# New planned step durations, leads and limits for the order of a graph network's last stage

## The chip, the cores and the metric

The kernel runs on one core of a Trainium2 chip. The metric is the device time of one execution in microseconds (us), taken as the median of several runs. A profile of one execution gives start and end of every instruction. PE is the matrix engine (TensorE), DVE is VectorE, ACT is ScalarE, POOL is GpSimd, SP is SyncE, which here issues most DMAs. Each engine works through its own list of instructions in order; semaphores make one engine wait for another. PSUM is the small memory that PE writes to, SBUF the large one.

## What is computed

128 graphs of 128 nodes with 128 features pass through four layers of graph networks. Each layer normalizes its input, applies a relu, attends over the graph's edges and adds the result to its input:

```
h = relu(layernorm(x));  x = x + L0(h, adj)
    y = softmax(where(adj > 0, scores(|x_i - x_j|), -9e15)) @ x
    y = leaky(batchnorm(y @ Wg.T + bg), 0.01);  out = [x, y] @ Wt.T + bt
h = relu(layernorm(x));  x = x + L1(h, adj)
    8 heads of 32:  att = softmax(where(mask, leaky(f1_i + f2_j, 0.2), -9e15))
    xc = elu(att @ h_head);  h2 = xc @ W2
    one more attention over h2;  out = elu(att2 @ h2) + h
h = relu(layernorm(x));  x = x + L2(h, adj)
    one attention on h itself;  out = elu(att @ h)
h = relu(layernorm(x));  x = x + L3(h, adj)
    typed scores src_i a[edge type] dst_j;  out = softmax(leaky(scores)) @ val @ pw.T + pb
```

## The kernel before

Earlier stages (until about 1724 us of the profile) compute the pairwise differences of layer 0, its two batch statistics and its attention, and leave in DRAM the values that the rest needs. The last stage, the function `layers_01`, is all the change is about. It is the arm for edges that are 0 or 1. It does the end of layer 0 and layers 1 to 3, for 32 groups of four graphs (`GC = 4`).

A group's work is a Python generator, `group(g)`, with helpers that it calls or forks. Every `yield` in it announces the next step: the engine, the planned duration in us, the buffers that the step takes, and those that are free after it. The code up to the next `yield` issues that step's instructions. The planner `in_order` keeps up to `Z_UNDER_WAY` such generators going, and at each turn picks the step that can begin first by the planned durations, plus a hand-over of 0.2 us between engines. A table `Z_LATER` shifts the rank of a kind of step by some us (a negative number puts it ahead). `Z_KEPT` says how many buffers of a kind have to stay free for the oldest group before a younger one may take one. What the planner picks becomes the fixed order of PE, ACT, DVE and POOL in the built program. The planned times have no other effect: on the chip each instruction starts when its engine reaches it and its semaphores are met.

The steps of one group, with the lines of the profile:

- Load: four DMAs on SP (L1808): `xg`, `yt`, `ht` with 3 buffers each, the edge mask with 10.
- Layer 0's end: ACT `yl` (L1919), DVE `leaky` (L584), PE (L1925, L1928), DVE sum `x1` (L1933).
- Three times `normal` and `transposed`: DVE statistics (L1715, L1717), ACT (L1720, L1721), POOL two tensor_tensor (L1724, L1725), PE transposes (L1732), ACT copy with relu (L1735).
- Layer 1's heads: PE (L1948), DVE splits into two bf16 parts (L1957 to L1960), ACT five times (L1969), then for each of the four graphs PE scores `z` (L1821), ACT exps (L1827, L1830), DVE maximum and masking (L1832). For each pair of graphs PE `pv` (L1843), DVE `vals` (L1846), PE 64 small matmuls into `va` and `sm` (L1861), ACT (L1872, L1873), DVE `xT` (L1875). Then the elu: ACT (L1981, L1982), DVE (L1985).
- Layer 1's second attention and layer 2's attention, both in `single_head`: ACT exps (L1750 or L1747), DVE masking (L1740), PE weighted sums `po` (L1784), DVE reciprocal `ri` and product `xh` (L1791, L1793), DVE positive part plus the residual (L1774, in `positive`), ACT `ex` (L1763), DVE the sum `xo` (L1767). `own` (L2010) and `hv` (L1905) are small or medium DVE steps ahead of them. `x1h` (L1891) is the residual of layer 1.
- Layer 3: PE (L2043, L1882, L2056), ACT (L2046, L1885, L2058), PE `sel` and `other` (L2064), DVE choice by edge (L2066), ACT exps (L2069, L2070), DVE maximum (L2072), PE `po` (L1784), DVE `ri` and `xh`, POOL the sum (L2078), and the store by SP (L2079). POOL also adds the bias to the residual (L1814).

The buffers: four PSUM tiles `ps`, two double PSUM tiles `pz`, 30 SBUF tiles `t` of 128x512, 13 `w` of 128x1024, and smaller sets.

The planner's choice, in which the change acts by the numbers alone:

```
begin = max([free_at[engine], c["ready"], *(events[e] for e in c["after"])])
...
    spare = 0 if c["age"] == oldest else kept.get(kind, 0)
...
age = c["age"] if started < len(makers) else -c["age"]
rank = begin + later.get(c["key"], 0.0), age, k
```

Of the kernel before, what the change touches and what calls it, by code (L numbers as in the profile page):

```python
# [32 lines left out]
UNDER_WAY = 6  # L33
Z_UNDER_WAY = 8
Z_T, Z_W, Z_P, Z_F, Z_O, Z_M = 30, 13, 4, 4, 6, 10
Z_KEPT = {"t": 12, "w": 4, "vals": 1, "v": 3}
C_T, C_W, C_V, C_O, C_M = 28, 11, 3, 6, 7
# [32 lines left out]
Z_LATER = {  # L70
    "2": -0.5, "3": 0.3, "4": -1.2, "6": -0.3, "7": 1.5, "8": -0.4, "11": -0.4, "13": 0.3, "16":
    0.4, "21": -1.5, "25": -6.2, "28": -6.7, "29": -5.8, "32": -4.8, "34": -1.9, "36": -0.4,
    "38": -1.1, "39": 0.6, "40": -2.6, "43": 0.4, "45": -4.1, "46": -1, "47": -6.9, "48": 0.2,
    "49": -7.5, "55": -0.6, "56": 0.5, "57": -8, "58": -0.6, "59": -8, "62": -0.1, "63": 0.4,
    "0.0": -0.6, "14.2": 0.2, "14.3": -0.2, "14.4": -1.9, "14.6": -0.1, "14.0.1": -1, "14.1.2":
    -0.3, "15.3": -0.4, "15.5": -0.4, "15.6": -0.3, "15.0.1": -7.8, "15.0.2": -0.2, "15.1.1":
    0.4, "15.1.2": -0.2, "20.0": -2.2, "37.0": -0.5, "42.0": -0.1, "50.0": 4.4, "53.0": 0.2,
    "53.1": -0.2, "54.1": 0.3,
}
# [126 lines left out]
def kernel(ctx: ExitStack, tc: tile.TileContext, x, adj, w, out):  # L206
# [1468 lines left out]
    def layers_01(first_in):  # L1675

        with tc.tile_pool(name="c_in", bufs=3) as c_in, tc.tile_pool(
# [31 lines left out]
            def normal(x, out):  # L1709

                yield DVE, 1.1, "", ""
                s6 = c_s.tile([P, GC, 6], F32, tag="s6", name="s6")
                mv = c_s.tile([P, GC, 2], F32, tag="mv", name="mv")
                for g in range(GC):
                    nc.vector.bn_stats(s6[:, g, :], x[:, g, :])  # L1715
                for g in range(GC):
                    nc.vector.bn_aggr(mv[:, g, :], s6[:, g, :])  # L1717
                yield ACT, 0.47, "", ""
                rs = tile_s("rs")
                nc.scalar.activation(rs, mv[:, :, 1], AF.Ln, bias=eps_c)  # L1720
                nc.scalar.activation(rs, rs, AF.Exp, scale=-0.5)  # L1721
                yield POOL, 2.1, "t", ""
                xn = tile_t("xn")
                nc.gpsimd.tensor_tensor(xn, x, bcast(mv[:, :, 0], 2, P), ALU.subtract)  # L1724
                nc.gpsimd.tensor_tensor(xn, xn, bcast(rs, 2, P), ALU.mult)  # L1725
                out.append(xn)

            def transposed(xn, out, frees):
                yield PE, 1.0, "ps", frees
                pt = psum("pt")  # L1730
                for g in range(GC):
                    nc.tensor.transpose(pt[:, g, :], xn[:, g, :], ident)  # L1732
                yield ACT, 0.5, "t", "ps"
                t = tile_t("hTc")
                nc.scalar.activation(t, pt, AF.Relu)  # L1735
                out.append(t)
# [5 lines left out]
            def single_head(z, own, mask, least, values, ones_at, after, out):  # L1742

                yield ACT, 1.02 if own else 0.57, "t", "ps"
                t = tile_t("p")
                if own is None:
                    nc.scalar.activation(t, z, AF.Exp, bias=shift_01, scale=1.0 - SLOPE)  # L1747
                else:
                    for g in range(GC):
                        nc.scalar.activation(  # L1750
                            t[:, g, :], z[:, g, :], AF.Exp, bias=own[:, g : g + 1], scale=1.0 - SLOPE
                        )
                yield DVE, 0.62, "", ""
                masked_larger(t.rearrange(flat), mask.rearrange(flat), least)
                yield "join",
                yield PE, 1.0, "pz", "t v"
                po = weighted(t, values, ones_at + 1)
                yield DVE, 0.86, "t", "pz"
                xh = over_sums(po, ones_at)
                yield "fork", positive(xh, after, out)  # L1760
                yield ACT, 0.53, "t", ""
                ex = tile_t("ex")
                nc.scalar.activation(ex, xh, AF.Exp)  # L1763
                yield "join",
                yield DVE, 0.62, "", "t t t"
                xo = out[0].rearrange(flat)
# [4 lines left out]
            def positive(xh, after, out):  # L1771
                yield DVE, 0.63, "t", ""
                xo = tile_t("xo")
# [38 lines left out]
            def with_bias3(x3):  # L1812
                yield POOL, 1.3, "", ""
                nc.gpsimd.tensor_tensor(x3, x3, bcast(pb_bc, 1, GC), ALU.add)  # L1814

            def head_attention(i, f1d, fl, mask, es, ps_):
                yield PE, 0.34, "pz w", ""
                z, p = psum2("z"), tile_w("p")
                for s in range(2):
# [4 lines left out]
                    )  # L1824
                yield ACT, 1.13, "", ""
                z = z.rearrange("p s (h j) -> p (s h) j", h=HH)
# [3 lines left out]
                nc.scalar.activation(z, z, AF.Exp, scale=1.0 - SLOPE)  # L1830
                yield DVE, 1.1, "", "pz"
                nc.vector.scalar_tensor_tensor(p, z, 1.0, bcast(mask[:, i, :], 1, NH), ALU.max, ALU.mult)  # L1832
                ps_[i] = p

            def two_graphs(k, f1d, fl, mask, h1T, es, xT):
# [3 lines left out]
                yield "join",  # L1839
                yield PE, 0.88, "ps vals", ""  # L1840
                pv = c_ps.tile([P, 2, NH * DH], F32, tag="ps", name="pv")
                for a in range(2):
                    nc.tensor.matmul(pv[:, a, :], h1T[:, 2 * k + a, :], w1c, start=True, stop=True)  # L1843
                yield DVE, 0.6, "", "ps"
                vals = c_v.tile([P, 2 * NH, DH], F32, tag="vals", name="vals", bufs=Z_P)
# [3 lines left out]
                )  # L1849
                yield PE, 2.05, "ps ps", "w w vals"  # L1850
                va, sm = (
                    c_ps.tile([P, 2, 2, P], F32, tag="ps", name=name) for name in ("va", "sm")
                )
                for a in range(2):
                    i = 2 * k + a
                    for s in range(2):
                        for to in (va, sm):
                            for h in range(HH):
# [9 lines left out]
                                )  # L1868
                yield ACT, 1.17, "t", "ps"
                r = tile_t("r")  # L1870
                rf = r.rearrange(flat)
                nc.scalar.activation(rf, sm.rearrange("p a s n -> p (a s n)"), AF.Ln)  # L1872
                nc.scalar.activation(rf, rf, AF.Exp, scale=-1.0)  # L1873
                yield DVE, 0.61, "", "ps t"
                nc.vector.tensor_tensor(  # L1875
# [3 lines left out]
            def type_scores(t, h3T, dstT, by_type):  # L1879
                yield PE, 0.82, "ps", ""  # L1880
                pp = psum("pp")
# [6 lines left out]
            def with_h1(xn, x1, res):  # L1888
                yield DVE, 0.89, "t", "t t"
                x1h = tile_t("x1h")  # L1890
# [5 lines left out]
            def scaled(ph2, h2):  # L1896
                yield ACT, 0.95, "", "pz"
                for i in range(GC):
# [4 lines left out]
            def relu_scaled(hv, xn):  # L1903
                yield DVE, 0.82, "", "t"
                nc.vector.scalar_tensor_tensor(  # L1905
# [3 lines left out]
            def group(g):  # L1909
# [5 lines left out]
                res = {}  # L1915
                yield ACT, 0.72, "t", ""
                xg, mask, yt, ht = loaded.pop(g)
                yl = tile_t("yl")
                nc.scalar.activation(yl, yt, AF.Identity, bias=y_bi, scale=y_sc)  # L1919
                yield DVE, 0.82, "", ""  # L1920
                leaky(nc.vector, yl.rearrange(flat), yl.rearrange(flat), 0.01)
                yield PE, 1.9, "ps", "t"
                po = psum("po0")
                for i in range(GC):
# [5 lines left out]
                    )  # L1930
                yield DVE, 0.66, "t", "ps " + in_slot
                x1 = tile_t("x1")
# [12 lines left out]
                for i in range(GC):  # L1945
                    for s in range(2):
# [4 lines left out]
                        )  # L1951
                yield DVE, 1.85, "", "ps"
                fa = c_v.tile([P, 2 * P], BF16, tag="fa", name="fa")
# [6 lines left out]
                nc.vector.scalar_tensor_tensor(f, fb, parts_m[:, 1:2], pff, ALU.mult, ALU.add)  # L1960
                yield ACT, 2.47, "f w", ""
                es = c_s.tile([P, GC, NH], F32, tag="es", name="es")
# [15 lines left out]
                yield "join",  # L1978
                yield ACT, 2.15, "w", "f t"
                u = tile_w("u")  # L1980
                nc.scalar.activation(u, xT, AF.Exp)  # L1981
                nc.scalar.activation(u, u, AF.Relu, bias=one, scale=-1.0)  # L1982
                yield DVE, 1.15, "", "w"
                uf, xf = (t.rearrange("p k n -> p (k n)") for t in (u, xT))
                nc.vector.scalar_tensor_tensor(uf, uf, -1.0, xf, ALU.mult, ALU.max)  # L1985

                yield PE, 2.1, "pz v", "w"
                h2 = tile_v("h2")
# [11 lines left out]
                yield "fork", scaled(ph2, h2)  # L2000
                yield PE, 0.95, "ps", ""
                z = psum("z2")
                for i in range(GC):
# [3 lines left out]
                    )  # L2007
                yield DVE, 0.35, "", ""
                own = tile_s("own")
# [8 lines left out]
                h2T = got.pop()  # L2018
                yield PE, 1.85, "ps", "t"
                z = psum("z3")  # L2020
                nc.tensor.matmul(z, a1bc, h2T, start=True, stop=False)
                for i in range(GC):
                    nc.tensor.matmul(
                        z[:, i, :], h2T[:, i, :], a2c.to_broadcast([P, P]), start=False, stop=i == GC - 1
                    )
                yield ACT, 0.15, "v", ""
                hv = tile_v("hv")
# [27 lines left out]
                for i in range(GC):  # L2055
                    nc.tensor.matmul(pv[:, i, :], h3T[:, i, :], vpw, start=True, stop=True)  # L2056
                yield ACT, 0.48, "", "ps"
                nc.scalar.copy(val[:, :, 0:P], pv)  # L2058
                yield "join",
                yield PE, 1.88, "ps ps", "t t"  # L2060
                sel, other = psum("sel"), psum("other")
# [8 lines left out]
                nc.scalar.activation(q, sel, AF.Exp, scale=SLOPE)  # L2070
                yield DVE, 0.76, "", "t"
                nc.vector.tensor_tensor(p, p, q, ALU.max)  # L2072
                yield PE, 1.0, "pz", "t v"
                po = weighted(p, val, P + 1)
                yield DVE, 0.86, "t", "pz"
                xh = over_sums(po, P)
                yield POOL, 1.45, "", "t t"
                nc.gpsimd.tensor_tensor(xh, xh, x3, ALU.add)  # L2078
# [510 lines left out]
```

## Time and profile before

| What | us |
|---|---|
| Median of 3 runs (2614.23 to 2618.11) | 2615.92 |
| The profiled execution's own time | 2615.94 |
| Its span, first to last instruction | 2614.1 |
| The last stage in it, from about 1724 to the last store | 890 |

Over the whole span PE is busy 93%, DVE 92%, ACT 83% and POOL 62%; in the last stage these shares differ, and only they count here. DMA is busy for 14% of the last stage. A group line of the profile names line, engine, operation, tiles and shapes, then the count, the busy time, the mean ns of one, and the idle time of the engine just before, with what ended it. DVE instructions overlap by some 80 ns in the records, so that the time from one start to the next is a little shorter than the duration that is shown.

Where a group is named by its number in the texts, its first output is computed in that order, 0 to 31. From group 8 to group 23 one group ends every 26.65 us.

### The profile page before, as it was taken

What the parts mean: (1) busy time and instruction counts of PE and PEld (TensorE: products, weight loads), DVE (VectorE), ACT (ScalarE), POOL (GpSimd) and SP (SyncE); (2) the same over time, 40 slices, a digit from 0 to 9 for tenths busy, and PEclk for the clock granted to TensorE, in tenths of its full rate; (3) what the DMA queues carried; (4) which work ended last, traced back from release to release, by engine and by line L of the source; (5) the groups of instructions that cost most, each with busy time, mean ns of one, the idle gap of its engine ahead of it and who ended that gap; (6) DMA issues with size and microseconds to landing.
All of it is one profiled execution on the core that took longest, in us unless ns stands there. A gap on an engine that the chain in (4) does not pass through costs nothing.

```text
span 2614.1 us, 51526 instructions
## 1 busy us (share of the span) xinstructions
PE 2434.2 (93%) x19584; PEld 1526.1 (58%) x19595; DVE 2410.7 (92%) x4638; ACT 2158.5 (83%) x3537; POOL 1633.1 (62%) x922
## 2 busy tenths in 40 slices
PE   7999999999999999799999999978888888898887
PEld 3443444444444443377787877756667777676766
DVE  9999999999999999698889888779899999999996
ACT  8999999999999999566666666558888888888875
POOL 8999999999999999654434444112333333333334
PEclk9999999999999999899999999989999999999999
DMA  3000000000000000232322232040011111111000
GB/s 106 25 25 25 25 25 25 25 25 25 25 25 25 25 21 9 79 100 94 98 86 85 93 97 70 15 146 10 27 48 46 48 46 48 38 56 38 14 10 27
DMA packets 135732, 122.62 MB, mean 47 GB/s; under 512 B 10865, under 2 KB 102450, under 8 KB 135474
## 3 DMA queue, kind: packets, MB, share of 16 engines
q1 hardware_dynamic: 134754, 118.89, 14.8%
q8 instruction: 158, 2.59, 0.4%
q14 instruction: 100, 0.82, 0.1%
q10 hardware_dynamic: 720, 0.33, 0.0%
HBM read 73.05 MB, written 46.14 MB: 46 GB/s over the span
## 4 chain that ended last, share of the span: by engine, by line
PE 48%; DVE 42%; ACT 5%; issue 3%; POOL 2%; DMA 0%; DVEq 0%; ACTq 0%; POOLq 0%
PE ph L789 19%; DVE d L759 9%; DVE six L801 7%; PE pl L1125 6%; DVE p L1832 5%; PE diff L1070 4%; PE ph L1083 3%; DVE s L1715 3%; DVE xh L1793 2%; PE sp L1093 2%; DVE p L1740 2%; DVE xo L1774 2%; DVE vals L1846 1%; DVE xT L1875 1%; DVE xo L1767 1%
## 5 line engine op out<-in xcount | busy, mean ns | idle before, releaser
L764 POOL TENSOR_TENSOR d<-he 128x2016 f32<-128x2016 f32 (+1 forms) x272 | 961.0, 3560 | 17.7 <-PE ph L789 15.1
L789 PE MATMUL ph<-d,w1T 128*64 128x512 f32 (+1 forms) x4096 | 912.4, 596 | 16.2 <-DVE six L801 9.8
L768 ACT ACTIVATE d<-d 128x2048 f32<-128x2048 f32 (+1 forms) x448 | 832.9, 1887 | 18.9 <-POOL d L764 17.8
L789 PEld LDWEIGHTS ph<-d,w1T 128*64 128x64 f32 x4096 | 323.2, 136 | 545.5 <-issue 471.0
L759 DVE SCALAR_TENSOR_TENSOR d<-pt,he 128x2048 f32<-128x2048 f32 x240 | 543.3, 2271 | 4.6 <-PE ph L789 4.4
L801 DVE BATCH_NORM_STATS2 six<-ph 128x6 f32<-128x512 f32 (+1 forms) x704 | 438.1, 677 | 11.7 <-PE ph L789 11.6
L1724 POOL TENSOR_TENSOR xn<-xo,mv 128x512 f32<-128x512 f32 x64 | 78.9, 1232 | 310.3 <-DVE mv L1717 243.2
L1056 POOL TENSOR_TENSOR base<-base,own_d 128x512 f32<-128x512 f32 x32 | 41.9, 1309 | 204.9 <-PE ph L1083 130.0
L795 ACT ACTIVATE ph<-ph 128x1008 f32<-128x1008 f32 x160 | 159.6, 998 | 11.1 <-PE ph L789 10.8
L1125 PE MATMUL pl<-its,it 128*128 128x128 f32 x1280 | 167.7, 279 | 0.0
L1079 ACT ACTIVATE d<-diff 128x640 f32<-128x640 f32 x128 | 90.0, 703 | 88.4 <-PE diff L1070 88.4
L1125 PEld LDWEIGHTS pl<-its,it 128*128 128x128 f32 x1280 | 152.8, 191 | 16.6 <-DVE s L1104 4.4
L1832 DVE SCALAR_TENSOR_TENSOR p<-z,mask 128x1024 f32<-128x1024 f32 x124 | 149.3, 1208 | 2.7 <-PE sm L1861 1.5
L1070 PE MATMUL diff<-inc,h 128*128 128x320 bf16 x768 | 128.4, 303 | 9.7 <-POOL h L1017 5.2
L1115 ACT CAST it<-pi 128x640 f32<-128x640 bf16 x128 | 86.4, 691 | 61.2 <-PE pi L1112 61.2
L1861 PE MATMUL va<-p,vals 128*32 128x128 f32 x2048 | 105.7, 277 | 29.8 <-DVE vals L1846 27.3
L1830 ACT ACTIVATE z<-z 128x1024 f32<-128x1024 f32 x128 | 129.0, 1008 | 4.1
L982 DVE SCALAR_TENSOR_TENSOR inc<-in_row,row 128x8 bf16<-128x8 f32 (+12 forms) x512 | 126.5, 315 | 0.3 <-PE in_row L973 0.2
L1725 POOL TENSOR_TENSOR xn<-xn,rs 128x512 f32<-128x512 f32 x96 | 120.0, 1250 | 8.8 <-ACT es L1827 1.0
L1724 POOL TENSOR_TENSOR xn<-x,mv 128x512 f32<-128x512 f32 x32 | 36.2, 1130 | 135.1 <-PE sm L1861 72.6
L1118 DVE TENSOR_TENSOR its<-pi,s 128x640 f32<-128x640 bf16 x128 | 101.9, 809 | 16.4 <-ACT it L1115 16.3
L2078 POOL TENSOR_TENSOR xh<-xh,xo 128x512 f32<-128x512 f32 x32 | 49.4, 1547 | 106.1 <-PE pt L1732 53.0
(326 smaller groups left out, 5234.8 us busy)
## 6 DMA issues: line engine op xcount, KB each, us to landing
ht<-h SPq DMA_DIRECT2D x64, 256.0 KB, 2.7
n<-ln_xn SPq DMA_DIRECT2D x32, 256.0 KB, 2.3
h<-he SPq DMA_DIRECT2D x32, 256.0 KB, 2.6
adj<-in_adj SPq DMA_DIRECT2D x32, 256.0 KB, 3.0
xn<-n SPq DMA_DIRECT2D x32, 256.0 KB, 2.6
xb<-in_x SPq DMA_DIRECT2D x32, 256.0 KB, 3.2
xb<-xb SPq DMA_DIRECT2D x32, 256.0 KB, 2.0
xg<-xb SPq DMA_DIRECT2D x32, 256.0 KB, 3.0
```

Of the source, the lines that this page charges most:

```text
L759: nc.vector.scalar_tensor_tensor(dv, own, 0.0, later, ALU.max, ALU.max if is_larger else ALU.subtract)
L764: nc.gpsimd.tensor_tensor(dv, later, own, ALU.subtract)
L768: nc.scalar.activation(d[:, 0 : 4 * n], d[:, 0 : 4 * n], AF.Abs, accum_out=sums[:, g, k : k + 1] if on_act else None,)
L789: nc.tensor.matmul(ph[64 * a : 64 * a + 64, t, 0:n], wt, x_, start=part == 0, stop=not is_larger or part == 3,)
L795: nc.scalar.activation(ph[:, :, 0:n], ph[:, :, 0:n], AF.Square, accum_out=squares[:, g, k : k + 1])
L801: nc.vector.bn_stats(six[g][:, 2 * by_bn.index((i, q)) + t, :], ph[:, t, 0:n])
L982: nc.vector.scalar_tensor_tensor(inc[:, :, e : e + n], in_row[:, :, 0:n], float(k + 1), row[:, :, 0:n], ALU.is_equal, ALU.subtract,)
L1070: nc.tensor.matmul(diff[:, a, 0 : SLOT_N // 2], h[:, i, :], inc[:, a * SLOT_N // 2 : (a + 1) * SLOT_N // 2], start=m == 0, stop=m == 2,)
L1125: nc.tensor.matmul(made["pl"][:, i, :], it[:, k, :], its[:, k, :], start=k == 0, stop=k == 4)
L1725: nc.gpsimd.tensor_tensor(xn, xn, bcast(rs, 2, P), ALU.mult)
L1830: nc.scalar.activation(z, z, AF.Exp, scale=1.0 - SLOPE)
L1832: nc.vector.scalar_tensor_tensor(p, z, 1.0, bcast(mask[:, i, :], 1, NH), ALU.max, ALU.mult)
```

## The change

Nothing but numbers of the planner change. No step, tile or buffer count is another.

- `Z_UNDER_WAY`: up to 11 groups at once instead of 8.
- `Z_KEPT`: the buffers held back for the oldest group: `t` 12 to 1, `w` 4 to 3, `v` 3 to 2, `vals` 1 to none, and one each of `ps`, `f` and `in`, which had none.
- `Z_LATER`: all shifts are new; their keys are places in a group's sequence of steps.
- The planned durations of most steps.

```diff
-Z_UNDER_WAY = 8
+Z_UNDER_WAY = 11
-Z_KEPT = {"t": 12, "w": 4, "vals": 1, "v": 3}
+Z_KEPT = {"ps": 1, "t": 1, "w": 3, "f": 1, "v": 2, "in": 1}
...
 Z_LATER = {
-    "2": -0.5, "3": 0.3, "4": -1.2, "6": -0.3, "7": 1.5, "8": -0.4, "11": -0.4, "13": 0.3, "16":
...
+    "1": 0.1, "4": -0.3, "6": 0.4, "7": 1.1, "8": -0.3, "9": -0.2, "11": -0.1, "13": 0.3, "16":
...
 def normal
-                yield POOL, 2.1, "t", ""
+                yield POOL, 2.35, "t", ""
 def transposed
-                yield PE, 1.0, "ps", frees
+                yield PE, 0.55, "ps", frees
 def single_head
-                yield ACT, 1.02 if own else 0.57, "t", "ps"
+                yield ACT, 1.13 if own else 0.63, "t", "ps"
-                yield DVE, 0.62, "", ""
+                yield DVE, 0.95, "", ""
-                yield DVE, 0.86, "t", "pz"
+                yield DVE, 0.8, "t", "pz"
-                yield DVE, 0.62, "", "t t t"
+                yield DVE, 0.7, "", "t t t"
 def positive
-                yield DVE, 0.63, "t", ""
+                yield DVE, 0.95, "t", ""
 def two_graphs
-                yield PE, 2.05, "ps ps", "w w vals"
+                yield PE, 1.87, "ps ps", "w w vals"
 def with_h1
-                yield DVE, 0.89, "t", "t t"
+                yield DVE, 0.62, "t", "t t"
 def relu_scaled
-                yield DVE, 0.82, "", "t"
+                yield DVE, 0.66, "", "t"
 def group
-                yield DVE, 0.82, "", ""
+                yield DVE, 0.66, "", ""
-                yield ACT, 2.15, "w", "f t"
+                yield ACT, 1.97, "w", "f t"
-                yield DVE, 0.35, "", ""
+                yield DVE, 0.2, "", ""
-                yield DVE, 0.76, "", "t"
+                yield DVE, 0.83, "", "t"
```

Some twenty more durations move by 0.01 to 0.18 us in the same way. In the old program DVE's instructions repeat themselves exactly, group after group, from group 8 to group 30. In the new one no two groups have the same surroundings; neighbouring groups often stand in pairs, with the same step of both back to back.

## The prediction

> **What bounds the kernel now.** The change touches only the last stage. I read first the busy time by stretches, cut where the picture changes: its start, its repeating middle, its end.
>
> ```profile
> 1724.00:1864.00 140.00, 114.26 (x1375) 91.87 (x1376) 120.83 (x269) 112.97 (x244) 38.39 (x33) 0.93 0.22 70
> 1864.00:2477.00 613.00, 540.88 (x6347) 432.35 (x6346) 585.67 (x1287) 513.24 (x1124) 233.04 (x207) 1.00 0.15 43
> 2477.00:2590.00 113.00, 100.20 (x1009) 77.34 (x1008) 97.83 (x221) 84.39 (x190) 48.78 (x43) 1.00 0.04 11
> 2590.00:2614.10 24.10, 13.52 (x105) 12.02 (x103) 8.58 (x16) 6.43 (x12) 6.15 (x6) 0.87 0.17 49
> ```
>
> Columns: length, then busy us of PE, weight loads, DVE, ACT, POOL; PE's granted clock; DMA. In the middle DVE is busy 585.67 of 613.00 us (95.5%), ACT 83.7%, POOL 38%. So DVE sets the pace. Its idle time by stretch is 19.2, 27.3, 15.2 and 15.5 us: 77 us, about 15 us of it hand-over gaps of under 0.25 us. I then asked what DVE's waits ended on, from 1724 us on (total us, times, longest):
>
> ```profile
> DVE ri L1791 <- PE po L1784: 20.5, 27, 1.3
> DVE sel L2066 <- PE other L2064: 11.6, 4, 8.5
> DVE x L1933 <- PE po L1928: 8.9, 7, 3.4
> ```
>
> The first is the middle's one wait, once per group; the second lies in the end, the third in the start. The timeline of DVE, and below it of POOL, over one period (start, duration):
>
> ```profile
> 2204.92 1.76 DVE L1740 SCALAR_TENSOR_TENSOR p<-p,mask 128x512 f32<-128x512 f32 x1
> 2206.61 0.68 DVE L584 SCALAR_TENSOR_TENSOR yl<-yl 128x512 f32<-128x512 f32 x1
> 2208.00 0.18 DVE L1791 RECIPROCAL ri<-po 128x4 f32<-128x4 f32 x1 [0.71 <-PE po L1784]
> ...
> 2219.87 1.52 DVE L1774 SCALAR_TENSOR_TENSOR xo<-xh,x1h 128x512 f32<-128x512 f32 x1
> ...
> 2231.59 1.76 DVE L1740 SCALAR_TENSOR_TENSOR p<-p,mask 128x512 f32<-128x512 f32 x1
> ```
> ```profile
> 2204.54 1.59 POOL L2078 TENSOR_TENSOR xh<-xh,xo 128x512 f32<-128x512 f32 x1 [3.77 <-PE pt L1732]
> ...
> 2219.48 1.37 POOL L1725 TENSOR_TENSOR xn<-xn,rs 128x512 f32<-128x512 f32 x1
> ```
>
> The period is 2231.59 - 2204.92 = 26.67 us, and 23 of them are the middle. After the masking (L1740) PE needs 1.32 us (2206.68 to 2208.00) before `ri`; one 0.68 us instruction covers it, 0.71 us stays idle. The second sight is that L1740 and L1774 take 1.76 and 1.52 us where they start while a POOL instruction runs. By groups (count | busy, mean ns | idle before):
>
> ```profile
> L1740 DVE SCALAR_TENSOR_TENSOR p<-p,mask 128x512 f32<-128x512 f32 x62 | 74.6, 1205 | 0.2 <-ACT p L1750 0.2
> L1774 DVE SCALAR_TENSOR_TENSOR xo<-xh,x1h 128x512 f32<-128x512 f32 x32 | 43.1, 1345 | 0.1
> L2072 DVE TENSOR_TENSOR p<-p,q 128x512 f32<-128x512 f32 x32 | 29.7, 929 | 2.4 <-ACT q L2070 2.4
> L1774 DVE SCALAR_TENSOR_TENSOR xo<-xh,xo 128x512 f32<-128x512 f32 x32 | 22.6, 708 | 0.1
> ```
>
> The undisturbed duration is 0.69 us. Mean less 0.69, times count: 32.1 + 21.0 + 7.6 + 0.6 us, with L1767, L1905, L584 and L1891 about 70 us in all: collisions with POOL cost as much as all DVE waits.
>
> **The change part by part.** No instruction is added, removed or resized: the same 8,800 or so stand in both programs, with 25 us of DVE time per group. Only their order on each engine changes. I laid DVE's instructions in both orders, gave each its mean start-to-start time in the profile (0.60 for a free 128x512, 1.20 for L1740, 1.14 for 128x1024, 1.06 for one normalization's statistics), and summed what stands between the two ends of each round trip through another engine.
>
> *Waits in the middle.* `ri` needs 1.32 us after the second masking. Old order: 25 of 32 groups have too little between, and the trace shows 17.7 us for it. New order: 8 groups are short, by 3.4 us together. Gain 14.3 us, taken off the path since DVE sets the end. The `ri` of the third attention (needs 1.25 after L2072): short by 1.1 us before, 6.0 after, nearly all of it in the last five groups. Scores from `leaky` to `x1` (2.96): 6.9 before, 7.7 after. The nine other round trips that are short anywhere (L1846 to L1875, L1960 to L1832, L2066 to L2072, L1717 to L1905 and to L1957, and such) together fall from 14.6 to 7.2. Sum: -14.3 + 4.9 + 0.8 - 7.4 = -16.0 us. How far such sums can be trusted: for the old order they give 36.8 us, where all DVE waits of the trace but those for L2066 come to 44. Most covers grow with eleven groups to choose from: L2010 to the first L1740 was 4.2 us in the middle and is now 3 to 46. The instructions late next are the five last groups' L2072 and `ri`.
>
> *End.* From the last statistics to `sel` takes at least 18.4 us (group 31). Between them DVE had 5.2 us of other work in the old order; the last group of the new (27) has 8.3. That would give 3.1 us, but five groups instead of four end together, and group 30 took 25.6 us in that crowd. I take 0, bounds -3 and +3.
>
> *Queues.* My sums let PE and ACT serve at once. The old order repeats itself group for group, so their queues fit once fitted; the new one never repeats. Nearest rows: ACT's five L1969 take 2.5 us in a piece, PE's 64 L1861 about 1.9. If one DVE instruction per group waits half of the old 0.71 us, 32 x 0.36 = 11 us; if none, 0. I take +4, since ACT has 16% idle in the middle.
>
> *Collisions.* Of the seven kinds that can collide, 112 instructions of 320 took over 0.85 us, costing 0.63 us each (70.8 / 112). By position in the order I get 114 for the old program, and 140 for the new (129 to 154 with POOL's starts shifted by up to 2 us). 26 more would cost 16 us. But if I sum the rest of the POOL instruction running when each one begins (1.04 us undisturbed, as L1724 at 2218.36), the old order gives 71.5 and the new 60 to 87, with mean 71. I take +2, bounds -11 and +16.
>
> The Trainium skill, "SBUF — State Buffer", section "SBUF: two separate sides", states that DVE instructions with two SBUF inputs and GpSimd ones hold the shared port as an exclusive lock for the whole instruction, the loser blocking fully. The 1.52 us of L1774 agree. The rule speaks against this change: the planner books one mean (0.95 us) for what is 0.69 or up to 1.76. By it alone, 26 new losers that each wait for a whole instruction would be +27 us, and the sum a loss of about 15.
>
> *Moved DMAs.* With 11 groups under way instead of 8, SP's loads shift. The mask has 10 buffers: in the new order at least 28 us pass from one's release to its next use, against 2.2 us to land. The others have at least 7.4 us against 3.0. POOL's queue: from statistics to L1905 takes 8.6 us; the smallest cover is 9.2. I cost these at 0; without that cover each would be a wait of its landing time, once.
>
> Sum: -16 + 0 + 4 + 2 = -10 us. The profiled execution took 2615.94 us (span 2614.1, 1.8 around it), the median of the runs is 2615.92: the same. So 2606.
>
> **The rivals.**
>
> *The wait moves (no change).* Queues take 11 and the end 3: -16 + 11 + 3 + 2 = 0, so 2616. For it: no engine's work falls, ACT is 84% busy. Against it: nearly all covers grow well beyond what a 0.7 us slip eats. This is also the case in which the plan's durations don't fit: it books 0.95 us for L1740, whose rows say 0.69 or 1.76.
>
> *Collisions decide (slower).* For it: L1767 collided 6 times of 64 in the trace, and in the new order 28 of them stand where POOL runs. With 26 more in all at a whole POOL instruction of 1.04 us, 27 us, against -16 + 4: +15, so 2631. It decides from 12 us, some 19 more at 0.63. Against it: places drawn at random would give less than the trace has, since POOL's 8 x 1.04 us fill 0.31 of a period and half an instruction is left on average: 320 x 0.31 x 0.52 = 52 us.
>
> *All of it (much faster).* Queues 0, collisions -11: 2616 - 16 - 11 = 2589.
>
> **How the numbers follow.** About 0.2%, 5 us, is what a measurement here can tell from no change. Forecast (2597 to 2611) 0.48, all of it 0.10, wait moves 0.17, collisions 0.25. Faster 0.58, same 0.17, slower 0.25. The bounds of the terms, all at their low and all at their high ends, are -16 - 3 + 0 - 11 = -30 and -16 + 3 + 11 + 16 = +14, so 2586 and 2630; they hardly come together, so 8 in 10 lie in 2589 to 2626. The forecast's own range is 2597 to 2611.
>
> **What would show it.** Right: `ri` waiting on `po` falls from 20.5 to under 9 us; DVE over 97% busy in the middle, with no period; L1740's mean near 1.1 and L1767's up from 0.76, all seven kinds together 60 to 87 us over 0.69. Wrong: DVE waits of more than 1 us on ACT's `z`, `u` or `f1d` in the middle, or an excess over 85 us. A start stretch longer than 150 us would mean that eleven groups at once jam the queues, which I costed at nothing.

## The result

The changed kernel takes 2606.31 us (median of 6 runs, 2604.11 to 2609.11) against 2614.85 us before (6 runs, 2614.11 to 2618.11). The ratio is 0.9965, 95% interval 0.9954 to 0.9975. The predicted time, 2606, is met to 0.3 us. What the trace shows behind it is not what was predicted. All waits together were forecast at -12 us (-16 + 0 + 4) and rose by 10.7; collisions were forecast at +2 us and fell by 20.2. Two terms were wrong with opposite signs and cancelled, so that the time was met this closely is luck.

The profiled execution of the changed kernel took 2609.11 us (span 2607.3), 6.8 less than the one of before. Its last stage, cut at the same times as before (length, then busy us of PE, weight loads, DVE, ACT, POOL; PE's clock; DMA):

```profile
1724.00:1864.00 140.00, 116.49 (x1549) 94.06 (x1551) 122.90 (x273) 109.87 (x235) 31.52 (x29) 0.87 0.26 80
1864.00:2477.00 613.00, 567.09 (x6408) 446.44 (x6399) 578.89 (x1290) 523.89 (x1147) 230.52 (x206) 0.99 0.13 39
2477.00:2590.00 113.00, 105.27 (x843) 82.69 (x842) 89.85 (x221) 81.41 (x182) 56.68 (x51) 1.00 0.06 17
2590.00:2607.30 17.30, 5.87 (x42) 5.10 (x40) 4.85 (x10) 3.07 (x6) 4.60 (x3) 0.69 0.19 53
```

In the middle DVE is busy for 578.89 of 613.00 us: 94.4%, where it was 95.5%, and where over 97% was forecast. So DVE waits more than before, not less. PE's granted clock in the first stretch is 0.87, where it was 0.93, but DVE's idle time there fell, from 19.2 to 17.1 us. Its waits in the last stage (total us, times, longest):

```profile
DVE ri L1791 <- PE po L1784: 18.9, 26, 1.8
DVE sel L2066 <- PE other L2064: 9.2, 9, 3.6
DVE x L1933 <- PE po L1928: 8.4, 5, 3.4
DVE hv L1905 <- ACT hv L2028: 6.8, 10, 1.3
DVE p L1832 <- ACT z L1830: 6.1, 13, 1.6
DVE vals L1846 <- PE pv L1843: 4.8, 6, 2.2
DVE xT L1875 <- ACT r L1873: 4.5, 9, 1.6
```

The first was 20.5 us and should have come under 9. `sel` fell from 11.6 and `x` from 8.9. Below them stand waits on ACT and PE that before were small (`xT` 1.9 us; `hv`, the masking L1832 on `z`, and `vals` 1.0 each). What became cheaper is DVE's own instructions. The groups that can collide with POOL (count | busy, mean ns | idle before):

```profile
L1740 DVE SCALAR_TENSOR_TENSOR p<-p,mask 128x512 f32<-128x512 f32 x62 | 47.0, 764 | 0.0
L1774 DVE SCALAR_TENSOR_TENSOR xo<-xh,x1h 128x512 f32<-128x512 f32 x32 | 24.2, 759 | 0.3
L1774 DVE SCALAR_TENSOR_TENSOR xo<-xh,xo 128x512 f32<-128x512 f32 x32 | 30.6, 963 | 0.1
L1767 DVE SCALAR_TENSOR_TENSOR xo<-ex,xo 128x512 f32<-128x512 f32 x64 | 50.6, 797 | 1.6 <-ACT ex L1763 0.5
L2072 DVE TENSOR_TENSOR p<-p,q 128x512 f32<-128x512 f32 x32 | 26.1, 816 | 2.4 <-ACT q L2070 2.3
L584 DVE SCALAR_TENSOR_TENSOR yl<-yl 128x512 f32<-128x512 f32 x31 | 28.8, 941 | 0.0
L1891 DVE SCALAR_TENSOR_TENSOR x1h<-xn,x 128x512 f32<-128x512 f32 x32 | 30.0, 939 | 0.0
...
L1985 DVE SCALAR_TENSOR_TENSOR u<-u,xT 128x1024 f32<-128x1024 f32 x32 | 43.3, 1352 | 2.6 <-ACT u L1982 2.5
...
L2010 DVE TENSOR_SCALAR own<-g 128x4 f32<-128x4 f32 x32 | 10.9, 339 | 0.0
```

The masking L1740 fell from a mean of 1205 ns to 764: 74.6 to 47.0 us, the largest single gain of the change. L1774 after `x1h` fell from 1345 to 759. Five kinds that hardly collided before do now: L584, L1891 and L1774 after `xo` (710, 708 and 708 ns before), and L1985 and L2010 (1232 and 238 before), which the prediction did not count.

Over the whole stage, from DVE's first instruction of it to its last:

| us | before | changed | difference |
|---|---|---|---|
| length | 881.6 | 875.9 | -5.7 |
| DVE busy | 813.0 | 797.2 | -15.8 |
| DVE idle | 68.6 | 78.7 | +10.2 |
| waits of over 0.25 us, with 2.85 just ahead of the first instruction | 55.8 | 66.5 | +10.7 |
| collisions: time over 0.69 us of the seven kinds | 70.8 | 50.6 | -20.2 |
| of 320 instructions, those over 0.85 us | 112 | 75 | -37 |

The collisions can be read instruction by instruction. DVE's timeline of the changed kernel, and below it POOL's (start, duration):

```profile
2096.76 0.68 DVE L1774 SCALAR_TENSOR_TENSOR xo<-xh,x1h 128x512 f32<-128x512 f32 x1
2097.96 1.15 DVE L1905 SCALAR_TENSOR_TENSOR hv<-xn,hv 128x512 f32<-128x512 f32 x1 [0.52 <-ACT hv L2028]
2099.03 1.53 DVE L1767 SCALAR_TENSOR_TENSOR xo<-ex,xo 128x512 f32<-128x512 f32 x1
2100.48 0.68 DVE L584 SCALAR_TENSOR_TENSOR yl<-yl 128x512 f32<-128x512 f32 x1
```
```profile
2096.92 1.64 POOL L2078 TENSOR_TENSOR xh<-xh,xo 128x512 f32<-128x512 f32 x1 [1.47 <-DVE xh L1793]
2098.53 1.49 POOL L1724 TENSOR_TENSOR xn<-x,mv 128x512 f32<-128x512 f32 x1
```

L1774 comes first and takes its free 0.68 us, although POOL's L2078 begins inside it. L2078 pays: it ends at 2098.56, which is the end of L1774 (2097.44) plus its own undisturbed 1.04 us and a little. L1905 begins inside L2078 and ends 0.55 us after it. L1724 begins inside L1905 and ends 0.91 us after it, and L1767 ends 0.54 us after L1724 (2100.02). So whoever comes second waits until the other's instruction has ended, and shows this time as busy. Of all 112 slow instructions before and all 75 after, POOL's was the first. In 60 overlaps before and 44 after DVE's was the first, and it lost nothing.

### The profile page after: what moved, and what is told of

It is laid out like the page before. It is cut to its first block, busy times and chain, and to the rows that moved or that the text cites. A ratio compares the mean times of both kernels' runs of the same rounds, so it can differ in the third digit from the quotient of the medians.

```text
span 2607.3 us, 51594 instructions
## 1 busy us (share of the span) xinstructions
PE 2460.5 (94%) x19595; PEld 1540.8 (59%) x19595; DVE 2394.9 (92%) x4638; ACT 2160.4 (83%) x3537; POOL 1630.7 (63%) x922
## 5 line engine op out<-in xcount | busy, mean ns | idle before, releaser
L789 PE MATMUL ph<-d,w1T 128*64 128x512 f32 (+1 forms) x4096 | 911.1, 595 | 16.6 <-DVE six L801 9.8
L1725 POOL TENSOR_TENSOR xn<-xn,rs 128x512 f32<-128x512 f32 x96 | 113.6, 1183 | 185.3 <-ACT rs L1721 173.3
L1724 POOL TENSOR_TENSOR xn<-xo,mv 128x512 f32<-128x512 f32 x64 | 77.4, 1209 | 159.9 <-DVE mv L1717 106.8
L795 ACT ACTIVATE ph<-ph 128x1008 f32<-128x1008 f32 x160 | 159.7, 998 | 11.0 <-PE ph L789 10.8
L1125 PEld LDWEIGHTS pl<-its,it 128*128 128x128 f32 x1280 | 152.8, 191 | 16.6 <-DVE s L1104 4.4
L1832 DVE SCALAR_TENSOR_TENSOR p<-z,mask 128x1024 f32<-128x1024 f32 x124 | 148.6, 1213 | 6.9 <-ACT z L1830 6.1
L2078 POOL TENSOR_TENSOR xh<-xh,xo 128x512 f32<-128x512 f32 x32 | 46.2, 1444 | 125.9 <-DVE xh L1793 86.5
L1118 DVE TENSOR_TENSOR its<-pi,s 128x640 f32<-128x640 bf16 x128 | 101.8, 808 | 16.4 <-ACT it L1115 16.3
L1087 ACT ACTIVATE z<-ph,h_bi,h_sc 128x320 f32<-128x320 f32 x128 | 77.6, 618 | 36.9 <-PE ph L1083 36.4
```

Of the source, the lines that this page charges most:

```text
L789: nc.tensor.matmul(ph[64 * a : 64 * a + 64, t, 0:n], wt, x_, start=part == 0, stop=not is_larger or part == 3,)
L795: nc.scalar.activation(ph[:, :, 0:n], ph[:, :, 0:n], AF.Square, accum_out=squares[:, g, k : k + 1])
L1125: nc.tensor.matmul(made["pl"][:, i, :], it[:, k, :], its[:, k, :], start=k == 0, stop=k == 4)
```

## The experiments

Unless a diff says otherwise, each kernel is one of the two. Each time stands with its ratio to the kernel before in the same batch of runs, and the 95% interval. "Stage", "waits" and "collisions" are the rows of the table above.

**Collisions taken away, in both orders.** The order of all steps is kept. POOL's tensor_tensor instructions of the last stage (L1724, L1725, L2078) work on 4 elements of a row, the one for the bias (L1814) becomes a memset of 4, and further memsets fill up their time; so normalization, bias and the last sum are not computed in full.

```diff
+MS, MS1 = 3, 2
...
-nc.gpsimd.tensor_tensor(xn, x, bcast(mv[:, :, 0], 2, P), ALU.subtract)
-nc.gpsimd.tensor_tensor(xn, xn, bcast(rs, 2, P), ALU.mult)
+nc.gpsimd.tensor_tensor(xn[:, :, 0], x[:, :, 0], mv[:, :, 0], ALU.subtract)
+nc.gpsimd.tensor_tensor(xn[:, :, 1], x[:, :, 1], rs, ALU.mult)
+for _ in range(MS):
+    nc.gpsimd.memset(xn[:, :, 2:P], 0.5)
```

In the order of before:

> The order of before, with POOL's tensor_tensor over 128x512 in the last stage (two for each normalization, the bias, the last sum) replaced by tiny ones on 4 elements a row and memsets that take about as long but read nothing; the values are then not the reference's. Theory A (gain of the change = fewer collisions, 71 to 55 us, eaten in part by 11 us more waits): L1740, L1774 and the others fall to 0.69 us, and since the waits grow when DVE comes earlier, the time falls by 40 to 65 us, not by the full 71. Theory B (collisions are only shown in DVE's records and cost the path nothing): within 10 us of before.

In the changed order:

> The same edit on the changed kernel. Theory A: without collisions the change has lost what it gained by, and its longer waits stay: at least as slow as e1, by 0 to 15 us. Theory C (the looser order with 11 groups under way is what gains, and the collisions only went along): faster than e1 by 5 to 15 us, as the changed kernel is faster than the one before.

| | us | ratio | stage | DVE busy | waits | collisions |
|---|---|---|---|---|---|---|
| old order | 2566.78 | 0.9808 (0.9792 to 0.9824) | 832.0 | 741.4 | 79.8 | 0.3 |
| new order | 2574.76 | 0.9841 (0.9824 to 0.9857) | 841.6 | 741.9 | 85.3 | 0.2 |

The masking (here L1743) in the old order, its durations as shortest/median/longest, and the memsets on POOL:

```profile
L1743 DVE SCALAR_TENSOR_TENSOR p<-p,mask x62: 658/684/693, 1796.7 to 2524.3; 128x512 f32<-128x512 f32 x62
```
```profile
L1728 POOL MEMSET xn<- 128x504 f32 x288 | 149.3, 518 | 11.1
```

62 maskings, none over 0.693 us: the 1.76 us of before came from POOL's tensor_tensor alone, and memsets do not cause it. Without collisions the new order is 8 us slower than the old. Theory A holds: all that the change gains, it gains from fewer collisions. As a plan of waits it is the worse one. B and C fall.

The second reading is what becomes of the waits. Old order, then new order:

```profile
DVE yl L585 <- ACT yl L1924: 20.7, 24, 0.9
DVE xo L1770 <- ACT ex L1766: 14.7, 24, 0.7
...
DVE ri L1794 <- PE po L1787: 5.9, 8, 1.3
```
```profile
DVE ri L1794 <- PE po L1787: 24.4, 38, 1.9
DVE p L1837 <- ACT z L1835: 11.4, 28, 1.7
```

In the old order, two waits appear that hardly existed, 24 times each and of 0.9 and 0.6 us on average; `yl` had waited for 3.0 us in all. The collided instructions ahead had covered them. `ri` falls from 20.5 to 5.9 us because `yl`, between the masking and `ri`, now does the waiting. All waits rise from 55.8 to 79.8 us in the old order and from 66.5 to 85.3 in the new. So 71 us of collisions cost the old kernel 49 us of time (2615.91 - 2566.78), and 51 cost the new one 32 (2606.31 - 2574.76, from two batches).

**Parts of the change.** The changed kernel with eight groups under way:

```diff
-Z_UNDER_WAY = 11
+Z_UNDER_WAY = 8
```

> The changed kernel with one part undone: 8 groups under way instead of 11; durations, shifts and held-back buffers stay the new ones, and the planner makes another order from them. Theory A (what decides is where DVE's two-input instructions and POOL's fall and how long the waits are in this one order; the shift table was searched for 11 groups and fits nothing else): slower than before by 10 to 50 us, with the collisions still 50 to 80 us and the waits 30 us or more longer. Theory F (the corrected durations are what makes the order better, the limit matters little): within 8 us of the changed kernel.

Measured: 2660.5 us, ratio 1.0164 (1.0143 to 1.0184): 44 us slower, as A had it, and F falls. Waits 104.5, collisions 56.3. One of its four executions took 6292.99 us; it is not in the ratio and stays unexplained.

The kernel of before with the new durations and `Z_KEPT`, but its old shifts and eight groups:

```diff
-Z_KEPT = {"t": 12, "w": 4, "vals": 1, "v": 3}
+Z_KEPT = {"ps": 1, "t": 1, "w": 3, "f": 1, "v": 2, "in": 1}
...
-                yield DVE, 0.62, "", ""
+                yield DVE, 0.95, "", ""
...
```

> The kernel before with the new durations and the new numbers of held-back buffers, but the old shifts and 8 groups. Theory F (the durations make the gain): 2600 to 2612 us. Theory A (durations, shifts and limits only work as one searched set): slower than before by more than 20 us, through waits, since the collisions of a scattered order are no more than some 70 us.

Measured: 2680.8 us, ratio 1.0256 (1.023 to 1.0282), 64 us slower; A holds. Its collisions are only 38.9 us, 12 less than the changed kernel's, but its waits are 127.0:

```profile
DVE sel L2066 <- PE other L2064: 22.8, 15, 8.1
DVE x L1933 <- PE po L1928: 22.7, 24, 3.4
DVE ri L1791 <- PE po L1784: 18.4, 23, 2.2
```

So the collisions are lower with the new durations and `Z_KEPT` in this order too, but that is worth nothing with the old shifts and eight groups.

**A planner that knows the port.** The port is what DVE and POOL hold in turn. If collisions are what the new order gained on, a planner that sees them should gain more. Here a step may name its parts that exclude the other engine's; DVE's planned durations are the undisturbed ones; a step that would begin inside POOL's part is ranked later; and shifts and limits are searched anew (10 groups).

```diff
-                yield POOL, 2.35, "t", ""
+                yield POOL, 2.08, "t", "", [1.04, 1.04]
...
-                yield DVE, 0.95, "", ""
+                yield DVE, 0.6, "", "", [0.6]
...
+            pen = 0.0
+            if port and shared and engine == DVE:
+                for a, b in held[POOL]:
+                    if a <= begin < b:
+                        pen = port * (b - begin)
-            rank = begin + later.get(c["key"], 0.0), age, k
+            rank = begin + pen + later.get(c["key"], 0.0), age, k
...
+            for part in shared[0]:
+                for a, b in held[POOL if engine == DVE else DVE]:
+                    if a <= done < b:
+                        done = b
+                held[engine].append((done, done + part))
+                done += part + (0.08 if engine == POOL else 0.0)
```

> A new order. The planner is given the undisturbed durations of the two-input DVE instructions (about 0.6 us from start to start), and lets such an instruction wait for a POOL tensor_tensor that is under way and the other way round, as the traces show it; a step that would have to wait ranks behind others that need not. 10 groups, shifts and held-back buffers searched anew. Theory A (collisions can be planned away, and cost the path most of what they show): the seven kinds' time over 0.69 us falls from 55 to below 35 us with waits no longer than the changed kernel's, so 2575 to 2595 us. Theory G (collisions and waits trade one for the other, so that any gain in one comes back in the other): 2603 to 2612 us.

Measured: 2593.15 us, ratio 0.9914 (0.9898 to 0.9931). Collisions 31.9 us (49 instructions), as expected; waits 75.7, more than the changed kernel's 66.5. Busy fell by 38.4 us against before and idle rose by 16.8. A holds in time and collisions, not in waits, and G falls; part of the gain went into waits here too.

The same planner, its durations set a little closer to the trace and `own` (L2010) counted among what collides, with `Z_LATER`, `Z_KEPT` and the eleven groups of the changed kernel:

```diff
-Z_UNDER_WAY = 10
-Z_KEPT = {"t": 4, "w": 1, "f": 1, "v": 3, "in": 2}
-Z_LATER = {"52": -5.3, "9": -21.5, "14.1.0": -0.2,
...
+Z_UNDER_WAY = 11
+Z_KEPT = {"ps": 1, "t": 1, "w": 3, "f": 1, "v": 2, "in": 1}
+Z_LATER = {"1": 0.1, "4": -0.3, "6": 0.4, "7": 1.1,
...
-Z_PORT = 2.0
+Z_PORT = 1.5
```

> The planner of e5 (it knows that two-input DVE instructions and POOL's hold each other up) with durations read once more from the traces of the changed kernel and e5, and the small own L2010 counted among those that collide; but 11 groups, shifts and held-back buffers are the changed kernel's, nothing is searched for. Theory H (knowing of the port is what gains): faster than the changed kernel, below 2600 us, with less than 35 us of collisions. Theory S (the search is what gains, the port is one thing among others): collisions below 35 us all the same, but waits over 80 us, and 2600 to 2625 us.

And that planner with these numbers searched again:

```diff
-Z_UNDER_WAY = 11
+Z_UNDER_WAY = 10
-Z_KEPT = {"ps": 1, "t": 1, "w": 3, "f": 1, "v": 2, "in": 1}
+Z_KEPT = {"t": 5, "f": 1, "v": 3, "in": 1}
-Z_LATER = {"1": 0.1, "4": -0.3, "6": 0.4, "7": 1.1,
...
+Z_LATER = {"9": -12.7, "14.1.0": -0.2, "44": -0.1, "23": -13.2,
...
-Z_PORT = 1.5
+Z_PORT = 2.0
```

> The planner and durations of e6, with shifts, held-back buffers and 10 groups searched for them. Theory S and theory A alike: collisions below 35 us and waits below e5's 76 us, so faster than e5 by 3 to 15 us: 2578 to 2590 us. Theory G (one trades for the other): 2590 to 2600 us.

Measured without a search: 2617.32 us, ratio 1.0004 (0.9995 to 1.0014); waits 83.0, collisions 46.1. That is what S has for time and waits, and H falls; the collisions, though, were not under the 35 that both expected. Searched again: 2591.56 us, ratio 0.9906 (0.989 to 0.9923); waits 62.3, collisions 35.8. That is within G's 2590 to 2600, at its low end, and S and A, with 2578 to 2590, miss. Against the changed kernel both waits and collisions are lower, so one was not traded for the other there; against the first version with the port the waits are 13.4 us lower and the collisions 3.9 higher. Of its waits:

```profile
DVE sel L2074 <- PE other L2072: 16.1, 8, 7.1
DVE ri L1799 <- PE po L1792: 13.7, 20, 1.7
DVE x L1941 <- PE po L1936: 7.3, 4, 3.4
```

This version beats both kernels: 24.7 us under before in its batch, and the interval of its ratio lies wholly below the changed kernel's. It is not clearly different from the first version with the port. The rule alone gained nothing; with a search it did. No run searched again without the rule, so how much of the gain is the search's own is not shown.

**ACT with less to do.** Many new waits are on ACT. If ACT's load made them, less work for it should take them away. One of the elu's two passes over `u` (L1982, 37 us of ACT in all) is left out, so the elu's `1 - u` and its relu are not computed.

```diff
-                nc.scalar.activation(u, u, AF.Relu, bias=one, scale=-1.0)
```

In the kernel before:

> The kernel before without ACT's second pass over u (L1982, 128x1024, 1.15 us, once per group), so 37 us less for ACT in its last stage, in the same order; the elu of layer 1 is then another function. Theory Q (in the middle of before DVE's waits are short round trips through PE, in the changed kernel they are queues on ACT and PE): no gain in the middle of before, since none of its 23 waits there is on ACT; 0 to 5 us in all, from the start and the end. Theory R (ACT at 84% slows both orders alike): 8 us or more.

In the changed kernel:

> The same edit on the changed kernel, whose middle has 12 us of waits on ACT, 10 of them with ACT busy until then. Theory Q: 4 to 10 us faster than the changed kernel, so 2596 to 2602 us, and more than e8 gains. Theory R: as much as e8 gains.

Measured: before 2613.88 us, ratio 0.9988 (0.9979 to 0.9998), 2.5 us less, with the middle's waits hardly changed (17.2 us, where they were 16.4). Changed 2606.23 us, ratio 0.9957 (0.9941 to 0.9974), against 2606.31 and 0.9965 for the changed kernel in another batch: no gain that the intervals tell from none. Its waits in the stage go from 66.5 to 63.4 us, and those in which ACT was busy until then, in the middle, from 9.9 to 8.0. Q misses for the changed kernel (4 to 10 us), and R had already missed for the one before (8 us or more). So 37 of ACT's 718 us less in this stage did not take these waits away. What is left is where ACT's and PE's steps stand in their orders, and PE's load: in the middle PE is busy for 567.09 of 613.00 us (92.5%), where it was 540.88 (88.2%). No run isolates either.

## Why the prediction was right, and where it was wrong

The waits were sorted for this by what the releasing engine did just before: idle (a round trip that DVE covered too little), or busy until then (its queue). This sorting is a reading of the traces, not a view of the profile.

- *What bounds the kernel:* right. DVE sets the pace in both; its busy time fell by 15.8 us and the runs by 8.5.
- *Waits in the middle, -16:* right in kind, some 5 us too large. Part of that is in the sum itself: it set the trace's 17.7 us for the old `ri` against its own 3.4 for the new one, but its own sums, 36.8 us in all for the old order, leave 14.2 for it (36.8 - 1.1 - 6.9 - 14.6). Like with like the gain is 10.8. Round trips too short for lack of cover went from 16.4 us to 5.4 (-11). The second masking's `ri`, which held 17.7 of the old 20.5 us, still waits for 7.4 (3.4 was forecast), and the third attention's for 9.3 (6.0 was forecast); that, with 1.6 at the first, is why the sum of `ri` stays near 19.
- *Queues, +4 (0 to +11):* the term that was mis-sized. In the middle, waits on an engine busy until then went from none to 16.6 us in 32 waits (ACT 9.9, PE 6.7), over the upper bound. "If one DVE instruction per group waits half of the old 0.71 us" was too little: 32 waits came, but of 0.52 us each on average, and some go over 1 us:

```profile
2065.26 0.16 DVE L2010 TENSOR_SCALAR own<-g 128x4 f32<-128x4 f32 x1
2067.06 1.23 DVE L1832 SCALAR_TENSOR_TENSOR p<-z,mask 128x1024 f32<-128x1024 f32 x1 [1.65 <-ACT z L1830]
```

  This wait of 1.65 us on `z` in the middle is the very sign the prediction named for being wrong. The reason it gave to be calm, "ACT has 16% idle in the middle", is no reason: 37 us less work for ACT gained nothing clear.
- *End, 0 (-3 to +3):* waits there rose by 4.8 us (20.1 to 24.9). The bound was too tight.
- *Collisions, +2 (-11 to +16):* the step that failed, with the wrong sign. Measured: -20.2 us for the seven kinds, about -13 with L1985 and L2010 (together 47.0 to 54.2 us of busy time), both outside the bounds. Its working has two faults. First, "by position in the order I get 114 for the old program" counted overlaps whoever came first, and met the true 112 by chance: 60 more overlaps were there, all free. This did not turn the sign: counted so, the traces have 172 and 119. Second, the other way, "the rest of the POOL instruction running when each one begins", did count only POOL's firsts and still gave 60 to 87 against 50.6, so the computed places of the new order were wrong in a way that shifting POOL's starts by up to 2 us does not cover. These places gave the wrong sign; how far off each was is not on record. "L1740's mean near 1.1" was 0.76; L1767's did go up, to 0.80.
- *Covers:* a fault in all sums of waits. They took each instruction's mean time with its collisions in it. A collision just ahead of a wait covers the wait, so the two terms cannot be added; the runs without collisions show 24 and 19 us of such overlap.
- *Small slips in the sums:* 62 maskings at 1205 ns make 31.9 us over 0.69, not 32.1, and 32 x 0.36 is 11.5, not 11. Nothing hangs on them.
- *Moved DMAs, 0:* right. None of the seven largest waits is on a load, and the start did not jam: DVE is busy 122.90 of the same first 140 us, 2 us more than before.
- *Rivals:* "the wait moves" was right in that `ri` stayed and waits on ACT came; "all of it" was right in that collisions fell, by more than the 11 us it had. Each came about in part, and together they gave the time, by luck. "Collisions decide" had the right lever and the wrong sign.

The Trainium skill, "SBUF — State Buffer", section "SBUF: two separate sides", has the lock as exclusive for a whole instruction and first come. The two timelines above agree, with 0.68 us for L1774, which came first, and 1.53 for L1767, which came second. The rule was not what failed; the places were that I put into it, which made it speak against the change.

Open: why the new order collides less. It was planned with one mean of 0.95 us for L1740 and L1774, not with POOL's times. The new durations with the old shifts collide less as well (38.9 us), with eight groups and the new shifts it is 56.3. No run shows whether more than chance is in it.

## What to carry to other kernels

A busy engine can hide waiting in its busy time: where one kind of instruction has two durations, look at what runs on the other engine at its start, and count only the cases in which the other came first. Such lost time and the waits behind it cover each other, so take one away in a run before adding up both; here 71 us of it were worth 49. In an order planned from durations, shifts and limits, these numbers are one set: parts of it alone cost 44 and 64 us, and what paid most was to give the planner the shared resource itself and search again, though how much the search alone would have given is open.

## What was not expected of the hardware

`own` (L2010), with one small SBUF input, waits for POOL too. The changed kernel's DVE, then POOL:

```profile
2118.99 0.66 DVE L2010 TENSOR_SCALAR own<-g 128x4 f32<-128x4 f32 x1
2119.56 0.68 DVE L1891 SCALAR_TENSOR_TENSOR x1h<-xn,x 128x512 f32<-128x512 f32 x1
```
```profile
2118.58 1.04 POOL L1724 TENSOR_TENSOR xn<-xo,mv 128x512 f32<-128x512 f32 x1 [9.90 <-DVE mv L1717]
```

It takes 0.66 us where its median is 0.16, ends when POOL does (2119.65 and 2119.62), and the next DVE instruction begins only 0.57 us after it. So not the number of inputs alone decides who is held.

Memsets on POOL hold nothing of the seven kinds (0.66 to 0.74 us in both runs with them, beside memsets of 0.52 us), but they do hold `own`. The changed order with memsets (`own` is L2015 there), DVE, then POOL:

```profile
2161.14 0.43 DVE L2015 TENSOR_SCALAR own<-g 128x4 f32<-128x4 f32 x1
```
```profile
2160.44 1.10 POOL L2085 MEMSET xh<- 128x508 f32 x2
```

`own` ends 0.03 us after the memsets (2161.57 and 2161.54). Ten of its 32 take 0.20 to 0.63 us in this run, and each ends 0.02 or 0.03 us after a memset does. But in nine of the ten the next DVE instruction begins 0.05 to 0.12 us after `own` has begun, so little is lost. The Trainium skill's same section lets a DVE instruction with two SBUF inputs contend only with GpSimd operations that read SBUF, which the seven kinds in these two runs agree with.
